# A two-layer image kernel: the LayerNorm of one image and the projection and convolution of the next, written as one stage

## The chip, the cores and the metric

The kernel runs on one core of one Trainium2 chip (trn2). The metric is the device time of one execution in microseconds (us); lower is better. Before the change the median of three runs is 33011.9 us (32997.37 to 33019.17). One execution was also recorded by the hardware profiler; it took 33035.09 us, of which 33033.3 us lie between the first and the last instruction (the span).

## What is computed

Eight images of 56x56 pixels with 192 channels pass through two layers, each of the form `x = x + layer(groupnorm(x))`. The first layer is not touched by the change. The second layer, cut to what matters here, is

```python
xz = x @ W_in.T                      # 192 -> 2*384
xc, z = split(xz, 2)                 # each 384 channels
xc = silu(depthwise_conv3x3(xc) + conv_b)
# eight directed scans over the 3136 pixels, each a recurrence with 16 states per channel
h  = exp(delta * A) * h + (delta * u) * B      ;  y_k = sum_n(h * C)
y  = sum over the 8 directions of y_k, put back in pixel order, + D * xc
y  = layernorm(y) * ln_w + ln_b
out = (y * silu(z)) @ W_out.T        # 384 -> 192
```

## The kernel before, in words

Everything is float32. After the first layer of all eight images, one loop over the images (`for b in range(B)`, L398) runs the second layer in three stages for each image. Each stage opens its own pools of on-chip memory and closes them again.

- **Preparation (L412 to L482).** The image is cut into seven tiles of 8 rows (448 pixels, `T`). For each tile the layer's input is loaded and normalised (`normed`, L400), projected to 3 blocks of 128 channels (`pp`, L432) and copied by ScalarE into a padded image `xp` (L435). Then the 3x3 depthwise convolution runs on TensorE: nine matmuls with diagonal matrices `dg` per block and tile (`pc`, L446), SiLU by ScalarE into a separate tensor `xc` (L453), a store of `xc` to DRAM (L459), and copies into the pixel orders that the scans read: `xo0` by VectorE (L470), `xo1` by GpSimd (L468), each with every second row reversed, and, once the whole image is there, the transposed order `xo2` by both (L481, L479). All are stored to DRAM (`xod`, L471, L482).
- **Scan (L485 to L923).** The long stage; its order is written by hand (`manual_schedule`, L500). VectorE runs the recurrences (L761). It is not changed. Its results go to DRAM (`ytd`, L709).
- **LayerNorm (L926 to L1040).** Again seven tiles. For each, four buffers `yk` of 112 pixels x 8 directions x 384 channels are loaded by 16 DMAs each, half issued on SP's queue and half on ScalarE's (L955, L967); three such buffers exist. TensorE transposes and adds them into `ysum` (L983, 24 instructions per buffer). VectorE adds `D*xc` (L994); TensorE forms the mean (`p1`, L999); VectorE subtracts it (L1002); ScalarE squares (L1004); TensorE forms the variance (`p2`, L1007); ScalarE takes the root (L1009), VectorE the reciprocal (L1010), then scales (L1024, L1025, L1028). TensorE forms the gate `pz` (L1014), ScalarE its SiLU (L1022). TensorE projects to 192 channels (`po`, L1032), VectorE adds the residual (L1039), SP stores the result (L1040).

In preparation and LayerNorm the framework's scheduler decides the order of the instructions on each engine; in the scan, and wherever `manual_schedule` is entered, an engine takes its instructions in the order in which the program writes them. An engine, and a queue that issues DMAs, works strictly in order: what waits holds up what stands behind it. Each DMA also waits, by a counter, for the eighth DMA before it.

A float32 matmul shows as two instructions in the trace, so 42 matmuls of `po` per image appear as 84.

Of the kernel before, what the change touches and what calls it, by code (L numbers as in the profile page):

```python
# [38 lines left out]
F32 = mybir.dt.float32  # L39
AF = mybir.ActivationFunctionType  # L40
ALU = mybir.AluOpType
# [43 lines left out]
def conv_kernel(ctx: ExitStack, tc: tile.TileContext, a: dict, out: bass.AP):  # L85
# [298 lines left out]
    xcd = [dram.tile([128, NB, L], F32, name=f"xc{b}") for b in range(B)]  # L384
# [9 lines left out]
    def halves(t):  # L394

        return t.rearrange("p d (h w) -> p d h w", w=HW)

    for b in range(B):  # L398
# [13 lines left out]
        with ExitStack() as st:  # L412
            one = st.enter_context(tc.tile_pool(name="prep1", bufs=1))
            pre = st.enter_context(tc.tile_pool(name="prep", bufs=2))
            pm = st.enter_context(tc.tile_pool(name="pp", bufs=4, space=PSUM))
            win = one.tile([CP, 2, 2 * DI], F32, name="win")
            nc.sync.dma_start(win, a["W_inT"])
            xp = [one.tile([128, HW + 2, HW + 2], F32, name=f"xp{d}") for d in range(NB)]
            dg = one.tile([128, NB, 9, 128], F32, name="dg")
            for d in range(NB):  # L420
                for edge in (xp[d][:, 0, :], xp[d][:, HW + 1, :], xp[d][:, :, 0], xp[d][:, :, HW + 1]):
                    nc.gpsimd.memset(edge, 0.0)  # L422
                for j in range(9):
                    nc.vector.tensor_scalar(
                        dg[:, d, j, :], ident, cw[:, d, j : j + 1], None, ALU.mult
                    )
            for t in range(NT):
                _, xn = normed(pre, t)
                for d in range(NB):
                    pp = pm.tile([128, T], F32, name="pp")  # L430
                    for c in range(2):
                        nc.tensor.matmul(  # L432
                            pp, win[:, c, d * 128 : (d + 1) * 128], xn[:, c], start=(c == 0), stop=(c == 1)
                        )
                    nc.scalar.copy(  # L435
                        xp[d][:, 1 + t * RT : 1 + (t + 1) * RT, 1 : HW + 1],
                        pp.rearrange("p (h w) -> p h w", w=HW),
                    )
            xc = one.tile([128, NB, L], F32, name="xc")
            xcv = xc.rearrange("p d (h w) -> p d h w", w=HW)  # L440
            for t in range(NT):
                for d in range(NB):
                    pc = pm.tile([128, RT, HW], F32, name="pc", tag="pp")
                    for j in range(9):
                        dy, dx = divmod(j, 3)
                        nc.tensor.matmul(  # L446
                            pc,
                            dg[:, d, j, :],
                            xp[d][:, t * RT + dy : t * RT + dy + RT, dx : dx + HW],
                            start=(j == 0),  # L450
                            stop=(j == 8),
                        )
                    nc.scalar.activation(  # L453
                        xc[:, d, t * T : (t + 1) * T],
                        pc.rearrange("p h w -> p (h w)"),
                        AF.Silu,
                        bias=cb[:, d : d + 1],
                    )
                nc.sync.dma_start(xcd[b][:, :, t * T : (t + 1) * T], xc[:, :, t * T : (t + 1) * T])  # L459
                for o in range(2):  # L460
                    xo = pre.tile([128, NB, T], F32, name=f"xo{o}")
                    for par in range(2):
                        src = xcv[:, :, t * RT + par : (t + 1) * RT : 2, :]
                        dst = halves(xo)[:, :, par::2, :]
                        if par != o:
                            src = src[:, :, :, ::-1]
                        if o:
                            nc.gpsimd.tensor_copy(dst, src)  # L468
                        else:
                            nc.vector.tensor_copy(dst, src)  # L470
                    nc.sync.dma_start(xod[b][o][:, :, t * T : (t + 1) * T], xo)  # L471
            xct = xcv.rearrange("p d h w -> p d w h")
            for t in range(NT):
                xo = pre.tile([128, NB, T], F32, name="xo2", tag="xo0")
                for par in range(2):
                    src = xct[:, :, t * RT + par : (t + 1) * RT : 2, :]
                    dst = halves(xo)[:, :, par::2, :]
                    if par:
                        nc.gpsimd.tensor_copy(dst, src[:, :, :, ::-1])  # L479
                    else:  # L480
                        nc.vector.tensor_copy(dst, src)  # L481
                nc.sync.dma_start(xod[b][2][:, :, t * T : (t + 1) * T], xo)  # L482
# [442 lines left out]

        with ExitStack() as st:  # L926
            one = st.enter_context(tc.tile_pool(name="ln1", bufs=1))
            wk = st.enter_context(tc.tile_pool(name="ln", bufs=2))
            pm = st.enter_context(tc.tile_pool(name="lnp", bufs=2, space=PSUM))
            py = st.enter_context(tc.tile_pool(name="lny", bufs=2, space=PSUM))  # L930
# [6 lines left out]
            for t in range(NT):  # L937
                pos = slice(t * T, (t + 1) * T)
                x1, xn = normed(wk, t)
                xc = wk.tile([128, NB, T], F32, name="xc")  # L940
                nc.sync.dma_start(xc, xcd[b][:, :, pos])

                ysum = py.tile([128, NB, 512], F32, name="ysum", tag="py")
                yv = ysum[:, :, :T].rearrange("p d (h w) -> p d h w", w=HW)
                for h0 in (0, 1, 4, 5):

                    yk = wk.tile([2 * HW, K, DI], F32, name="yk", bufs=3)
                    h = t * RT + h0
                    for place, o, rev in DIRS.values():
                        if o == 2:  # L950
                            continue
                        eng = nc.scalar if rev else nc.sync
                        for i in range(2):
                            at = (HW - 3 - h if rev else h) + 2 * i
                            eng.dma_start(  # L955
                                yk[i * HW : (i + 1) * HW, place], ytd[b][place, at * HW : (at + 1) * HW]
                            )
                    for rev in range(2):
                        for i in range(2):
                            for par in range(2):  # L960

                                at = HW + HW - 1 - h - 2 * i if par else h + 2 * i
                                if rev:
                                    at = L - 1 - (at + (HW // 2 - 1) * 2 * HW)
                                p0 = i * HW + par * (HW // 2)
                                eng = nc.scalar if rev else nc.sync
                                eng.dma_start(  # L967
                                    yk[p0 : p0 + HW // 2, 4 + 2 * rev : 6 + 2 * rev],
                                    ytd[b][
                                        4 + 2 * rev : 6 + 2 * rev, at : at + (HW // 2 - 1) * 2 * HW + 1 : 2 * HW  # L970
                                    ].rearrange("k l d -> l k d"),
                                )
                    for d in range(NB):
                        for place, o, rev in DIRS.values():
# [15 lines left out]
                            )  # L990

                y = wk.tile([128, NB, T], F32, name="y")
                for d in range(NB):
                    nc.vector.scalar_tensor_tensor(  # L994
                        y[:, d], xc[:, d], dsum[:, d : d + 1], ysum[:, d, :T], ALU.mult, ALU.add
                    )
                p1 = pm.tile([128, T], F32, name="p1", tag="pm")
                for d in range(NB):
                    nc.tensor.matmul(p1, ones, y[:, d], start=(d == 0), stop=(d == NB - 1))  # L999
                yc = wk.tile([128, NB, T], F32, name="yc")  # L1000
                for d in range(NB):
                    nc.vector.tensor_sub(yc[:, d], y[:, d], p1)  # L1002
                sq = wk.tile([128, NB, T], F32, name="sq")
                nc.scalar.activation(sq, yc, AF.Square)  # L1004
                p2 = pm.tile([128, T], F32, name="p2", tag="pm")
                for d in range(NB):
                    nc.tensor.matmul(p2, ones, sq[:, d], start=(d == 0), stop=(d == NB - 1))  # L1007
# [107 lines left out]
```

## Time and profile before

| | us |
|---|---|
| median of the runs | 33011.9 |
| profiled execution | 33035.09 |
| its span | 33033.3 |
| VectorE from the end of an image's last scan to the next image's first, seven times | 574.4 to 577.6 each |
| the last image's LayerNorm, from VectorE's last scan to the end of the span | 332 |
| TensorE, VectorE, ScalarE, GpSimd busy over the span | 30106.0, 23832.6, 23299.1, 22361.9 |

Every image shows the same pattern: some 3125 us of scan, in which all four engines are busy most of the time, and then a gap in which VectorE does no scan. The gap holds the LayerNorm of the image that was just scanned (about 329 us), then the preparation of the next one (about 206 us), then the start-up of the next scan (about 41 us). In the profile's groups of instructions, "busy" counts the time of an engine's instructions, "mean ns" is one instruction's duration (matmuls overlap each other, so their number times their mean exceeds the time that they take), and the last column is the time for which the engine idled just before them, with what ended it.

### The profile page before, as it was taken

How to read it: one execution, taken by the hardware profiler on the slowest of the kernel's cores; microseconds unless marked ns; L12 is line 12 of the kernel's file. 1: busy time of each engine (PE TensorE's matmuls, PEld its weight loads, DVE VectorE, ACT ScalarE, POOL GpSimd, SP SyncE). 2: the span in 40 equal slices, each digit the busy share in tenths (PEclk: the TensorE clock that was granted, in tenths of full speed). 3: DMA queues.
4: the chain of work that ended last, by engine and by line, in shares of the span. 5: the costliest groups of instructions: out<-in, count | busy, mean ns of one | idle time of the engine just before them, and what ended most of it. 6: DMA issues, size and time to landing. Idle time of an engine off the chain costs nothing. (4 is left out here: it accounts for less than half of the span.)

```text
span 33033.3 us, 535851 instructions
## 1 busy us (share of the span) xinstructions
PE 30106.0 (91%) x195376; PEld 20579.6 (62%) x195376; DVE 23832.6 (72%) x13236; ACT 23299.1 (71%) x63562; POOL 22361.9 (68%) x11632
## 2 busy tenths in 40 slices
PE   8999899979998899979998899979998899979998
PEld 5555566646665566646665566646665566646665
DVE  3444588848886588848886688848886688848886
ACT  2332588838886588838886688838885688838885
POOL 0000588838886588838886588838885688838885
PEclk9999999989999999989999999989999999989999
DMA  3222344444444444444444344444444344444444
GB/s 78 60 60 56 116 126 127 127 127 125 126 129 132 120 127 128 126 126 128 125 126 138 119 125 126 129 128 124 127 128 133 118 129 125 126 127 130 125 126 132
DMA packets 4719499, 3974.35 MB, mean 120 GB/s; under 512 B 3678496, under 2 KB 4401888, under 8 KB 4611008
## 3 DMA queue, kind: packets, MB, share of 16 engines
q1 hardware_dynamic: 4558272, 3778.58, 40.3%
q10 hardware_dynamic: 158592, 161.47, 1.9%
q8 instruction: 1552, 25.43, 0.3%
q14 instruction: 1083, 8.87, 0.1%
HBM read 3406.62 MB, written 547.17 MB: 120 GB/s over the span
## 5 line engine op out<-in xcount | busy, mean ns | idle before, releaser
L761 DVE TENSOR_TENSOR_SCAN h<-da,bx 128x1024 f32<-128x1024 f32 x9600 | 21447.9, 2275 | 3899.2 <-ACT bx L756 2956.6
L779 POOL TENSOR_TENSOR hc<-h,cbt 128x1016 f32<-128x1016 f32 x9600 | 20694.4, 2177 | 2470.8 <-DVE h L761 1973.9
L688 ACT ACTIVATE da<-delta,A_logs 128x254 f32<-128x254 f32 x39936 | 17115.8, 490 | 856.1 <-PE bx L733 807.1
L733 PE MATMUL bx<-bd,dut 63*128 63x252 f32 (+1 forms) x76800 | 11032.5, 404 | 1071.2 <-ACT bx L756 376.8
L789 PEld LDWEIGHTS yps<-ident,hc 128*127 128x127 f32 x76800 | 9246.5, 190 | 3384.3 <-issue 2081.0
L789 PE MATMUL yps<-ident,hc 128*127 128x128 f32 x76800 | 11065.2, 287 | 196.4 <-ACT bx L756 142.7
L733 PEld LDWEIGHTS bx<-bd,dut 63*128 63x128 f32 (+1 forms) x76800 | 6506.3, 187 | 4540.3 <-ACT da L688 878.0
L422 POOL MEMSET xp<- 128x58 f32 x96 | 10.3, 194 | 5692.5 <-DMA x<-x1d 3395.9
L612 POOL TENSOR_TENSOR du<-delta,xs 128x381 f32<-128x381 f32 x1600 | 1605.7, 1004 | 712.7 <-ACT bx L756 477.3
L1004 ACT ACTIVATE sq<-yc 128x1344 f32<-128x1344 f32 x56 | 74.0, 1322 | 2111.9 <-DMA yk<-yt 1781.2
L540 PE MATMUL px<-xs,xpw 128*64 128x508 f32 (+1 forms) x2688 | 1304.4, 576 | 226.7 <-DMA xs<-xo 198.4
L575 PE MATMUL pd<-pxs,dtw 13*128 13x508 f32 x2304 | 1296.6, 642 | 17.9 <-ACT delta L584 10.7
L584 ACT COPY delta<-pd 128x508 f32<-128x508 f32 x1152 | 669.7, 581 | 727.2 <-PE pd L575 721.4
L756 ACT COPY bx<-h 128x8 f32<-128x8 f32 x4608 | 753.2, 163 | 594.1 <-PE bx L733 324.2
L446 PE MATMUL pc<-xp,dg 128*128 128x448 f32 x3024 | 1138.0, 538 | 0.0
L774 ACT COPY carry<-h 128x8 f32<-128x8 f32 x4608 | 884.1, 192 | 320.9 <-DVE h L761 302.6
L756 ACT COPY bx<-carry 128x8 f32<-128x8 f32 x4992 | 820.4, 164 | 400.3 <-PE bx L733 369.1
L468 POOL COPY xo<-xc 128x672 f32<-128x672 f32 x112 | 80.6, 749 | 1392.8 <-issue 754.8
L699 ACT COPY yt<-yps 127x256 f32<-127x256 f32 (+1 forms) x2496 | 890.2, 357 | 175.6 <-PE yps L789 122.3
L446 PEld LDWEIGHTS pc<-xp,dg 128*128 128x128 f32 x3024 | 571.2, 189 | 565.5 <-issue 565.5
L470 DVE COPY xo<-xc 128x672 f32<-128x672 f32 x112 | 90.3, 848 | 1129.3 <-ACT xc L453 1129.3
L406 DVE TENSOR_SCALAR x1n<-x,gstat 96x448 f32<-96x448 f32 x224 | 103.6, 505 | 1078.8 <-DMA x<-x1d 803.5
(121 smaller groups left out, 17121.0 us busy)
## 6 DMA issues: line engine op xcount, KB each, us to landing
cbt<-cd SPq DMA_DIRECT2D x768, 2032.0 KB
bd<-bd SPq DMA_DIRECT2D x1600, 512.0 KB
xs<-xo SPq DMA_DIRECT2D x384, 762.0 KB
yt<-yt SPq DMA_DIRECT2D x1536, 190.5 KB
yk<-yt ACTq DMA_DIRECT2D x1792, 84.0 KB
yk<-yt SPq DMA_DIRECT2D x1792, 84.0 KB
xo<-xo SPq DMA_DIRECT2D x168, 672.0 KB
xc<-xc SPq DMA_DIRECT2D x112, 672.0 KB
```

The lines of the kernel that those rows point to most:

```text
L446: nc.tensor.matmul(pc, dg[:, d, j, :], xp[d][:, t * RT + dy : t * RT + dy + RT, dx : dx + HW], start=(j == 0), stop=(j == 8),)
L540: nc.tensor.matmul(self.px[:, : self.n], weights[self.k][0][:, d], self.xs[:, d], start=(d == 0), stop=(d == NB - 1),)
L575: nc.tensor.matmul(self.pd[:, : self.n], weights[self.k][1][:, d * 128 : (d + 1) * 128], self.pxs[0 : R + 1], start=True, stop=True,)
L612: nc.gpsimd.tensor_mul(self.du, self.delta[:, :, part], xs[:, :, part])
L688: yield nc.scalar.activation(da[:, : G.ncs, n, 1:], src.rearrange("p (c t) -> p c t", t=W), AF.Exp, scale=an[:, G.k, self.d, col : col + 1],)
L699: nc.scalar.copy(G.yt[:, : G.ncs, self.d * 128 : (self.d + 1) * 128], yps[:, self.i % 2, : G.ncs])
L733: mm = nc.tensor.matmul(self.bx[:, 4 * q : 4 * q + 4, 1 + 64 * r : 1 + 64 * r + nr], dut[rows, P.d * 128 : (P.d + 1) * 128], bd[rows, n0 : ...
L756: return nc.scalar.copy(self.bx[:, :, 0], prev)
L761: nc.vector.tensor_tensor_scan(self.h.rearrange("p n t -> p (n t)"), das[2 * (P.i % 2) + self.half][:, self.c].rearrange("p n t -> p (n t) ...
L774: nc.scalar.copy(P.carry[:, P.d, states(self.half)], self.h[:, :, W])
L779: nc.gpsimd.tensor_tensor(self.hc, self.h[:, :, 1:], G.cb[P.s][:, states(self.half), self.c * W : (self.c + 1) * W], ALU.mult,)
L789: nc.tensor.matmul(yps[:, self.P.i % 2, self.c], lhsT=self.hc[:, n], rhs=ident, start=(self.half == 0 and self.c == 0 and n == 0), stop=(s ...
```

## The change

The preparation stage remains for the first image only (`if b == 0`). The LayerNorm stage of image b now also holds the projection and the convolution of image b+1, and the whole stage stands under `manual_schedule`, so that its instructions run in the order written in the loop at its end. Besides:

- The convolution writes its result into the padded image itself, shifted by one pixel (`xcv = xp[:, :, :HW, :HW]`); the separate `xc` is gone.
- `xc` is no longer stored to DRAM (`xcd` is gone). The LayerNorm reads the order `xo0` in its place and turns every second row back while it adds, in six VectorE instructions of 224 pixels per channel block instead of three of 448.
- All loads of `yk` are issued on SP's queue; `load_y(j + 3)` is issued after the transposes of buffer j.
- The gate is formed block by block, the output projection of a tile is put into the next tile's turn, and LayerNorm works in place on `y`. In on-chip accumulator memory (PSUM) there is now one `ysum`, one bank for the two sums, two for gates and output, two for projection and convolution.

```diff
-    xcd = [dram.tile([128, NB, L], F32, name=f"xc{b}") for b in range(B)]
...
+        if b == 0:
             with ExitStack() as st:
...
+            st.enter_context(tc.manual_schedule())
+            more = b + 1 < B
...
+            class Next:
+                def load(self, t):
+                    if more and t < NT:
+                        self.xn = wk.tile([CP, 2, T], F32, name="xnext")
+                        nc.sync.dma_start(self.xn, x1d[b + 1][:, :, t * T : (t + 1) * T])
...
+                def orders(self, t):
...
+                            if o:
+                                nc.gpsimd.tensor_copy(dst, src)
+                            else:
+                                nc.vector.tensor_copy(dst, src)
+                def store(self, t):
+                    if more:
+                        for o in range(2):
+                            nc.sync.dma_start(xod[b + 1][o][:, :, t * T : (t + 1) * T], self.xo[o])
...
-                        eng = nc.scalar if rev else nc.sync
...
+                        nc.sync.dma_start(
+                            yk[i * HW : (i + 1) * HW, place], ytd[b][place, at * HW : (at + 1) * HW]
+                        )
...
+            X = Next()
+            tiles = [Tile(t) for t in range(NT + 1)]
+            X.load(0)
+            load_y(0)
+            tiles[0].load()
+            load_y(1)
+            X.normed(0)
+            X.project(0)
+            X.load(1)
+            load_y(2)
+            X.normed(1)
+            X.project(1)
+            X.load(2)
+            for t in range(NT):
+                Y, Z = tiles[t], tiles[t - 1] if t else None
+                Y.normed()
+                X.normed(t + 2)
+                Y.turn_back(0)
+                X.project(t + 2)
+                X.load(t + 3)
+                tiles[t + 1].load()
+                Y.turn_back(1)
+                X.conv(t, 0)
+                Y.gate(0)
+                Y.gate(1)
+                Y.turn_back(2)
+                Y.turn_back(3)
+                Y.with_x()
+                if Z:
+                    Z.project()
+                X.conv(t, 1)
+                Y.centre()
+                Y.gate(2)
+                if Z:
+                    Z.store()
+                X.conv(t, 2)
+                Y.scale()
+                X.orders(t)
+                X.store(t)
+            X.turned_order()
+            Y.project()
+            Y.store()
```

What the names of the loop stand for: `X` is the next image. `X.normed` is two VectorE instructions as in L406; `X.project` is the 12 instructions of L432 for one tile with three copies as in L435; `X.conv(t, d)` is one block's nine matmuls (18 instructions) as in L446 with its SiLU; `X.orders` and `X.store` are L470, L468 and L471; `X.turned_order` is L481, L479 and L482. `Y` is the tile of the present image. `turn_back(i)` is 24 instructions as in L983; `gate(d)` is one block of L1014 (4 instructions) with its SiLU; `with_x` is the six additions; `centre` is the 6 instructions of `p1`, the three subtractions and the squares; `scale` is the 6 instructions of `p2`, the root, the reciprocal and the scaling. `Z` is the tile before; `Z.project` is its 12 instructions of `po` with two additions on VectorE. For the last image `more` is false and all of `X` is empty.

## The prediction

> **What bounds the kernel now.** First the page: busy times, and VectorE (DVE) in the 40 slices.
>
> ```profile
> PE 30106.0 (91%) x195376; PEld 20579.6 (62%) x195376; DVE 23832.6 (72%) x13236; ACT 23299.1 (71%) x63562; POOL 22361.9 (68%) x11632
> ...
> DVE  3444588848886588848886688848886688848886
> ```
>
> The scan slices read 8; the slices of 4 to 6 between them are where the change works. So I went to the timeline of VectorE around the last of these gaps (start us, length us, instruction, idle before):
>
> ```profile
> 28989.57 10.97 DVE L761 TENSOR_TENSOR_SCAN h<-da,bx 128x1024 f32<-128x1024 f32 x5
> 29000.63 0.17 DVE L936 MEMSET ones<- 128x128 f32 x1
> ...
> 29533.17 1.42 DVE L481 COPY xo<-xc 128x672 f32<-128x672 f32 x1 [1.89 <-DMA xo<-xo]
> 29576.75 2.29 DVE L761 TENSOR_TENSOR_SCAN h<-da,bx 128x1024 f32<-128x1024 f32 x1 [42.16 <-ACT bx L756]
> ```
>
> One gap lasts 29000.5 to 29576.7, 576.2 us; the seven gaps differ by 3 us. The table by stretches says what TensorE (PE) does in its two parts, LayerNorm and then preparation with scan start-up (the columns are PE, weight loads, DVE, ACT, POOL busy, granted clock, DMA share, GB/s), and below them in one stretch of transposes:
>
> ```profile
> 29000.50:29329.40 328.90, 206.22 (x940) 124.19 (x940) 91.53 (x121) 40.96 (x36) 2.33 (x2) 0.80 0.56 151
> 29329.40:29576.70 247.30, 196.00 (x498) 96.01 (x498) 33.47 (x62) 37.72 (x64) 25.39 (x42) 0.85 0.35 117
> 29161.20:29168.40 7.20, 7.20 (x75) 7.02 (x73) 1.08 (x1) 0.00 (x0) 0.00 (x0) 1.00 0.54 156
> ```
>
> In LayerNorm TensorE idles 123 us and runs at a granted clock of 0.80; VectorE and ScalarE are nearly empty. The groups of TensorE in those stretches give the work:
>
> ```profile
> L983 PE MATMUL ysum<-ident,yk 112*128 112x112 f32 x672 | 73.4, 268 | 31.0 <-DMA yk<-yt 30.8 <-issue 0.2
> L1032 PE MATMUL po<-yc,wout 128*96 128x448 f32 x84 | 49.4, 759 | 59.6 <-DVE yc L1028 59.6
> L1007 PE MATMUL p<-sq,ones 128*128 128x448 f32 x42 | 29.1, 858 | 23.5 <-ACT sq L1004 23.5
> ...
> L446 PE MATMUL pc<-xp,dg 128*128 128x448 f32 x378 | 142.2, 538 | 0.0
> ```
>
> `pc` never waits: 142.2/378 = 0.376 us per instruction of 448 columns at full clock. `po` needs 49.4/84 = 0.59 because it starts slow after a wait. The timeline of one LayerNorm tile shows the chain:
>
> ```profile
> 29141.40 4.13 PE L1007 MATMUL p<-sq,ones 128*128 128x448 f32 x6 [3.19 <-ACT sq L1004]
> ...
> 29154.04 7.29 PE L1032 MATMUL po<-yc,wout 128*96 128x448 f32 x12 [8.52 <-DVE yc L1028]
> 29161.17 7.26 PE L983 MATMUL ysum<-ident,yk 112*128 112x112 f32 x74
> ```
> ```profile
> 29146.23 2.95 DVE L1010 RECIPROCAL rs<-rs 128x448 f32<-128x448 f32 x1 [6.30 <-ACT rs L1009]
> ...
> 29152.34 1.56 DVE L1028 TENSOR_TENSOR yc<-yc,sz 128x1344 f32<-128x1344 f32 x1
> ```
>
> From the end of `p2` (29145.53) to the end of the scaling (29153.90) pass 8.4 us in which TensorE does nothing; and `po`, 12 instructions, then takes 7.29 us where 12 x 0.376 = 4.5 would do. An idle spell of 8.5 us so costs 2.8 us more by the clock. Transposes take 7.26/74 = 0.098 us, 24 of them 2.35.
>
> Last, SP's queue while buffers come free one at a time:
>
> ```profile
> 29163.67 2.04 SPq L955 DMA_DIRECT2D yk<-yt  x4
> 29166.90 2.14 SPq L967 DMA_DIRECT2D yk<-yt  x4
> ```
>
> That is 0.52 us to issue one load of `yk`.
>
> **The merged tile, part by part.** TensorE's work per tile is 4 x 2.35 transposes, 4.5 projection (12), 20.3 convolution (54), 4.5 gate (12), 4.5 `po` (12), 4.5 `p1` and `p2`: 47.7 us, 334 for seven tiles, against 535 for LayerNorm and preparation (329 + 206). The waits of LayerNorm for `sq` lie under a convolution block (6.8), and the wait of `po` for the scaling under the next tile's start. That is the gain.
>
> What the written order takes back is on VectorE. At a tile's end stand, in order, the scaling of this tile, two copies of `X.orders`, `Y.normed` and `X.normed(t + 2)`; on TensorE `X.project(t + 2)` stands second in the next tile, after 2.35 us of transposes. So `X.project` waits for all of them: 8.4 (above) + 1.6 (two copies, row L470, 0.85 each, overlapped) + 0.9 + 0.9 (L406, 0.5 each) = 11.8 us after `p2`. TensorE idles 9.5 us and pays the 2.8 us of the clock again, as `po` does now. Behind the waiting projection are the second transposes, all convolutions and gates: nothing covers it. A tile with projection and a predecessor takes 47.7 + 9.5 + 2.8 = 60.0; there are four (t = 1 to 4).
>
> Tiles 5 and 6 have no projection: 43.2. There SP decides: its two `X.store` wait for the VectorE copies (10.0 after the tile's start), and `load_y` of the fourth buffer stands behind them: two stores 1.1, 16 x 0.52 = 8.3, landing 2.9 (as `out_y<-x` at 29326.40 freed its waiter at 29329.37): 22.3. TensorE is there after 3 x 2.35 + 6.8 + 3.0 = 16.9, waits 5.4, pays some 2 of clock: 50.5, two of them 101. In tiles 1 to 4 TensorE gets to that buffer only at 33, so this wait is covered by the other.
>
> Start (from the last scan): the last `yt` store lands at 13.9; weights, the first x and its norm to 21; `X.project(0)` at slow clock 7.3 to 29; `X.load(1)` stands on SP behind two buffers and two tile loads (34.5), lands 37.4, norm 38.3, `X.project(1)` slow again to 45.7; first transposes 48; `X.project(2)` 52.6; then 2.35 + 6.8 + 3.0 + 4.7 + 6.8 + 2.3 + 1.5 + 6.8 + 2.3 to 89. End: scaling and copies 10.0, seven transposed copies paced by their stores as now (29516.1 to 29534.6) 18; then a new step: the last `po` additions (1.1), the `out` store and its landing stand ahead of the scan's first load on SP, 4.4 where it was 1.0; start-up 41.2 as now. Sum 73.6. The gap becomes 89 + 240 + 101 + 73.6 = 504, 72.6 less than 576.2; seven of them: -508.
>
> The last image's LayerNorm (332 us) now has all loads on SP: 64 x 0.52 + 3 x 0.55 = 35 per tile against 41.2 (29154.04 to the next `po` at 29195.29): 6 x 6 less, some 15 more at its start, where four buffers come through one queue: -20, between -40 and +30. Sum: 33035.1 - 528 = 32507 for the profiled execution, which was 23.2 above the median: 32485.
>
> **Costs that the trace does not show.** One queue loading alone: between 0.32 us (an issue's own length) and 0.94 (at this stage's start SP issued 32 loads from 29015.63 to 29045.81, but ScalarE as many beside it). I take 0.52, since the new loop frees one buffer at a time, as that row does; even 0.88 would fit under 60 us. The six additions of 224 pixels take between 2.0 and 4.0 us (half of, or the whole of, 0.67 each); they lie under `po` and a convolution (11.3), so nothing either way. The dropped `xc` store saves SP 0.5 us per tile: nothing on the path. ScalarE has some 10 us per tile (SiLU 6 x 0.63, copies 3 x 0.54, square 1.32, root 0.63, two table loads 1.28): covered.
>
> The Trainium skill speaks against the order on one point: "TensorE: Matmul & The Clock Gate", Part 4 on PE-mode transpose, says that transposes do not count as activity for the clock gate. By that rule 4.7 us of transposes ahead of `Z.project` would let the clock fall in each tile, 2.8 us x 49 = 137 us in all. The stretch above was 7.2 us of transposes at a granted clock of 1.00, and ten `pz` instructions after it took 3.94 us (0.39 each): I count nothing; by the rule it would be 32620.
>
> **The rivals.** (1) TensorE sets the pace: if the projection did not wait, four tiles lose 12.3 us each, 344 us over seven gaps: 32140. For it: VectorE would have 17 us of work in 48. Against it: the order of instructions, in which the norm stands behind the scaling. (2) SP's pace near 0.75: start +11 (48 loads), tiles 5 and 6 +3.7 each (16 loads), seven times 18.4, and the last image +50 instead of -20: 32685. (3) Slower: one queue needs 1.0 us per load. Then SP's 64 loads and its other DMAs (3.3 us) set the tile at 67 us. With d per load the gap is 89 - 25 (48 start loads at 0.52) + 6 x 3.3 + 73.6 = 157, plus (48 + 6 x 64) d = 432 d: 589, or +13 seven times; the last image's six tiles take 65.6 each instead of 41.2, +146: about +240, 33250. It decides from d = 0.93 on. For it: 0.94 at the start; against it: 0.52 whenever ScalarE's queue is not pressing too. (4) Nothing moves because the parts still run one after another: the order of instructions excludes it almost wholly.
>
> **Chances.** Forecast (32400 to 32570) 0.62; rival 1 and what lies between, 0.10; rival 2 (32600 to 32850) 0.20; rival 3, 0.06; no change 0.02. The range 32240 to 32720 leaves out the lower half of rival 1, the upper third of rival 2, and 3 and 4. A measurement tells 0.2% (66 us) from no change: faster 0.92, same 0.03, slower 0.05.
>
> **What would show it.** In the profile after: VectorE's gap near 504; TensorE's `pp` group with some 9.5 us idle before it four times per gap, released by the norm on VectorE; the clock in the merged stage above 0.85; `ysum` waiting for `yk` only in tiles 5 and 6 and at the start; SP's loads near 0.52. Wrong if `ysum` waits for `yk` in every tile (rival 2 or 3), or if `pp` does not wait (rival 1).

## The result, and the profile after

The changed kernel takes 32435.45 us (32433.44 to 32446.73) where the kernel before took 33009.24 us in the same series: a ratio of 0.9827, 95% interval 0.981 to 0.9844. The profiled execution took 32433.44 us, 601.7 less than the one before. Seven gaps gave 542.4 of it (497.3 to 500.1 us each, where they were 574.4 to 577.5), the last image's LayerNorm 53.4 (278.6 against 332.0), the scans, whose code is the same, some 16, with a cause that stays open; the first layer, which the change does not touch, took 10.3 us more.

The page's busy times and VectorE's slices, after:

```profile
PE 29974.2 (92%) x195376; PEld 20574.4 (63%) x195376; DVE 23854.0 (74%) x13460; ACT 23290.3 (72%) x63667; POOL 22357.6 (69%) x11632
...
DVE  3444588858887588848887688848886688858886
```

They hardly differ from before: TensorE runs as many instructions. A gap of 500 us is less than one slice of 811 us, so the page can't show this change. The stretches of the last gap can (start, the four tiles with a projection, the two without, the end, and last the whole gap; the third number from the right is the granted clock):

```profile
28531.10:28619.10 88.00, 60.64 (x228) 35.21 (x229) 13.12 (x46) 12.27 (x19) 5.12 (x16) 0.81 0.58 164
28619.80:28859.30 239.50, 202.84 (x795) 117.41 (x794) 64.44 (x101) 38.13 (x53) 5.76 (x8) 0.90 0.49 143
28859.30:28960.40 101.10, 91.99 (x365) 54.76 (x363) 30.52 (x47) 15.87 (x20) 3.62 (x5) 0.93 0.37 113
28960.40:29028.90 68.50, 24.41 (x48) 9.58 (x48) 19.61 (x19) 11.91 (x21) 13.27 (x16) 0.60 0.63 191
...
28531.10:29028.90 497.80, 380.58 (x1438) 217.65 (x1438) 127.70 (x211) 78.83 (x113) 27.77 (x44) 0.85 0.50 147
```

The prediction had 89, 240, 101 and 73.6 for these four; it counted from the ends of `p2`, 0.7 us ahead of the reciprocals at which these rows begin, so that the measured end is 69.2. In the merged tiles the clock is 0.90 and 0.93, above the 0.85 that it named. TensorE idles 117 us of the gap, where it idled 174. TensorE's groups over this gap say where:

```profile
L998 PE MATMUL pc<-xp,dg 128*128 128x448 f32 x378 | 145.7, 538 | 0.0
L1123 PE MATMUL ysum<-ident,yk 112*128 112x112 f32 x672 | 73.7, 268 | 8.4 <-DMA yk<-yt 8.4
L980 PE MATMUL pp<-xnext,win 96*128 96x448 f32 x84 | 50.5, 773 | 62.8 <-DVE xnext L965 36.7 <-DMA yk<-yt 26.1
L1193 PE MATMUL po<-y,wout 128*96 128x448 f32 x84 | 35.8, 579 | 8.7 <-DVE y L1187 8.7
```

`po` waits once, at the end, and no longer in every tile (59.6 us before). The projection of the next image, `pp`, waits 36.7 us for the norm, and this is four times one wait, as TensorE's timeline shows (last column: the idle time before):

```profile
28551.07 7.71 PE L980 MATMUL pp<-xnext,win 96*128 96x448 f32 x12 [16.44 <-DMA yk<-yt]
28568.48 7.54 PE L980 MATMUL pp<-xnext,win 96*128 96x448 f32 x12 [9.70 <-DMA yk<-yt]
...
28630.57 7.23 PE L980 MATMUL pp<-xnext,win 96*128 96x448 f32 x12 [9.16 <-DVE xnext L965]
28690.03 8.22 PE L980 MATMUL pp<-xnext,win 96*128 96x448 f32 x12 [9.16 <-DVE xnext L965]
28750.47 7.02 PE L980 MATMUL pp<-xnext,win 96*128 96x448 f32 x12 [9.17 <-DVE xnext L965]
28809.72 8.11 PE L980 MATMUL pp<-xnext,win 96*128 96x448 f32 x12 [9.17 <-DVE xnext L965]
```

What stands ahead of that norm on VectorE, in the first of these tiles:

```profile
28626.17 1.56 DVE L1187 TENSOR_TENSOR y<-y,sz 128x1344 f32<-128x1344 f32 x1
28627.65 1.60 DVE L1024 COPY xo<-xp 128x672 f32<-128x672 f32 x2
28629.17 0.92 DVE L1096 TENSOR_SCALAR x1n<-x,gstat 96x448 f32<-96x448 f32 x2
...
28630.01 0.93 DVE L965 TENSOR_SCALAR xnext<-xnext,gstat 96x448 f32<-96x448 f32 x2
```

The end of the scaling, the copies, one norm, the other: `pp` begins at 28630.57, when the first half of the last one is there. In tiles 5 and 6 SP decides. SP's queue and then TensorE in tile 5 (SPq is the queue of SP):

```profile
28868.76 1.49 SPq L1029 DMA_DIRECT2D xo<-xo  x2
28870.36 5.59 SPq L1060 DMA_DIRECT2D yk<-yt  x8
28876.00 3.42 SPq L1071 DMA_DIRECT2D yk<-yt  x8
```
```profile
28875.57 0.29 PE L1123 MATMUL ysum<-ident,yk 112*128 112x112 f32 x1 [0.29 <-DMA yk<-yt]
...
28881.32 3.56 PE L1123 MATMUL ysum<-ident,yk 112*128 112x112 f32 x18 [1.19 <-DMA yk<-yt]
28884.71 4.69 PE L1193 MATMUL po<-y,wout 128*96 128x448 f32 x12
```

The loads stand behind the two stores of the next image, and the fourth transposes trickle in behind them.

### The profile page after: what moved, and what is told of

The parts are those of the page before. It is cut to its first block, busy times and chain, and to the rows that moved or that the text cites. A ratio compares the mean times of both kernels' runs of the same rounds, so it can differ in the third digit from the quotient of the medians.

```text
span 32431.7 us, 535874 instructions
## 1 busy us (share of the span) xinstructions
PE 29974.2 (92%) x195376; PEld 20574.4 (63%) x195376; DVE 23854.0 (74%) x13460; ACT 23290.3 (72%) x63667; POOL 22357.6 (69%) x11632
## 5 line engine op out<-in xcount | busy, mean ns | idle before, releaser
L732 PEld LDWEIGHTS bx<-bd,dut 64*128 64x128 f32 (+1 forms) x76800 | 6510.0, 187 | 4511.0 <-ACT da L687 876.4
L1022 POOL COPY xo<-xp 128x672 f32<-128x672 f32 x98 | 70.5, 749 | 2841.8 <-ACT xp L1005 2841.8
L1005 ACT ACTIVATE xp<-pc,conv_b 128x448 f32<-128x448 f32 x147 | 93.5, 636 | 1352.1 <-PE pc L998 1352.0
L998 PE MATMUL pc<-xp,dg 128*128 128x448 f32 x2646 | 1019.5, 538 | 0.0
L1142 DVE SCALAR_TENSOR_TENSOR y<-xc,dsum,ysum 128x224 f32<-128x224 f32 x336 | 125.4, 443 | 1132.3 <-PE ysum L1123 1132.3
L620 ACT COPY dut<-pt 127x384 f32<-127x384 f32 x1600 | 757.9, 474 | 167.5 <-PE pt L616 123.6
L616 PE MATMUL pt<-ident,du 128*127 128x128 f32 x4800 | 815.7, 279 | 52.1 <-POOL du L611 36.2
```

What stands on the lines that cost most here:

```text
L732: mm = nc.tensor.matmul(self.bx[:, 4 * q : 4 * q + 4, 1 + 64 * r : 1 + 64 * r + nr], dut[rows, P.d * 128 : (P.d + 1) * 128], bd[rows, n0 : ...
L998: nc.tensor.matmul(pc, dg[:, d, j, :], xp[:, d, t * RT + dy : t * RT + dy + RT, dx : dx + HW], start=(j == 0), stop=(j == 8),)
```

## The experiments

Theory A is the prediction's: TensorE's work is 47.7 us per merged tile, and the change gives part of its gain back at two places in in-order queues, the norm behind the scaling on VectorE and the `X` store ahead of the loads on SP. Its main rival says that another resource stands right behind (loads, VectorE's sum of work), so that moving these instructions gives nothing. The medians below are of four runs, eleven for the split loads; each stands beside runs of the kernel before on the same chip. These took between 33004.8 and 33071.9 us, so that across rows the ratios compare better than the times. Periods are from one tile's reciprocal to the next one's, in the last gap. None of the kernels changes what is computed.

| | us | ratio to before, interval | a gap (mean of seven) | tiles 1 to 4 | tiles 5, 6 | last LayerNorm |
|---|---|---|---|---|---|---|
| before | 33009.24 | 1 | 576.2 | | | 332.0 |
| the change | 32435.45 | 0.9827 (0.981 to 0.9844) | 498.7 | 59.9 | 50.6 | 278.6 |
| X's norm ahead | 32141.01 | 0.9733 (0.9719 to 0.9748) | 456.7 | 48.9 | 51.4 | 278.5 |
| two queues | 32519.06 | 0.9849 (0.9834 to 0.9863) | 505.3 | 59.9 | 49.2 | 315.9 |
| order alone | 32603.99 | 0.9874 (0.9858 to 0.9891) | 521.6 | | | 277.7 |
| X's store behind | 32364.44 | 0.9789 (0.9774 to 0.9803) | 483.3 | 59.7 | 43.1 | 277.6 |
| norms and store | 31995.69 | 0.969 (0.9675 to 0.9704) | 434.0 | 47.6 | 43.1 | 284.8 |
| start and end too | 31941.55 | 0.9676 (0.966 to 0.9692) | 428.3 | 47.6 | 43.1 | 284.7 |
| loads split | 33135.15 | 1.0021 (1.0012 to 1.003) | 565.8 | 63.9 | 63.5 | 468.8 |

**The norm of X ahead of the scaling.**

```diff
                 Y.normed()
-                X.normed(t + 2)
+                if t == 0:
+                    X.normed(2)
...
+                X.normed(t + 3)
                 Y.scale()
```

> The next image's norm of an X tile is issued on VectorE ahead of the scaling of the Y tile (the first one stays where it is), nothing else is moved. Theory A (VectorE's written order is what makes the projection wait, 9.16 us of idle time ahead of L980 in tiles 1 to 4): that wait goes, tiles 1 to 4 fall from 59.9 us to about 49 us (the 47.7 us of TensorE's work and some 1 us of wait for yk), a gap between scans from 498.7 to about 455 us, the kernel to about 32130 us. Rival R (the wait only passes on to the yk loads behind the store of X on SP's queue, or to the gate): tiles stay at 55 us or more, a gap at 480 us or more, the kernel at 32295 us or more.

32141 us, a gap of 456.7. TensorE's groups over the last gap:

```profile
L1123 PE MATMUL ysum<-ident,yk 112*128 112x112 f32 x672 | 74.6, 268 | 13.2 <-DMA yk<-yt 13.2
L980 PE MATMUL pp<-xnext,win 96*128 96x448 f32 x84 | 37.4, 600 | 28.0 <-DMA yk<-yt 17.5 <-DVE xnext L965 10.5
```

Of the 36.7 us none is left in tiles 1 to 4 (the 10.5 are at the start), and `pp` itself takes 37.4 us where it took 50.5: the slow restarts went with the waits. 11.0 us per tile, 44 in four, are the price of where two instructions of 0.5 us stood; 42.0 of them reach the gap, since tiles 5 and 6 become 0.8 us longer each. `ysum` waits only 4.8 us longer in the whole gap, so that little of the wait passed on to the loads.

**The store of X behind the next tile's loads.**

```diff
                 Y.turn_back(0)
+                if t:
+                    X.store(t - 1)
                 X.project(t + 2)
...
                 X.orders(t)
-                X.store(t)
+            X.store(NT - 1)
             X.turned_order()
```

> Only the store of X is moved, behind the first yk loads of the next tile; both norms stay behind the scaling. Theory A (two separate waits: VectorE's order in tiles 1 to 4, SP's order in tiles 5 and 6): tiles 1 to 4 stay at 60 us, tiles 5 and 6 fall from 50.5 to 44 or 45 us, a gap near 487 us, the kernel near 32350 us. Rival R (the yk wait of tiles 5 and 6 comes from the loads' own pace or from the three buffers, whatever stands ahead of them on SP): tiles 5 and 6 stay at 49 us or more, the kernel within 30 us of 32435 us.

Tiles 1 to 4 stay at 59.7, tiles 5 and 6 fall to 43.1, as much as TensorE's work. The gap is 483.3, 3.7 less than expected, for the most part because the wait in these tiles goes wholly. TensorE's groups:

```profile
L1123 PE MATMUL ysum<-ident,yk 112*128 112x112 f32 x672 | 67.5, 259 | 0.0
L980 PE MATMUL pp<-xnext,win 96*128 96x448 f32 x84 | 49.0, 753 | 63.9 <-DVE xnext L965 47.0 <-DMA yk<-yt 16.9
```

`ysum` waits for nothing, `pp` as in the change (four times 9.16 us; the other 10.4 for `xnext` lie at the start): two separate waits, each with its own place in a queue.

**Both norms and the store.** As the two above, and the next tile's `Y.normed` is also put ahead of the scaling.

```diff
-                Y.normed()
-                X.normed(t + 2)
+                if t == 0:
+                    Y.normed()
+                    X.normed(2)
                 Y.turn_back(0)
+                if t:
+                    X.store(t - 1)
...
+                X.normed(t + 3)
+                if t + 1 < NT:
+                    tiles[t + 1].normed()
                 Y.scale()
                 X.orders(t)
-                X.store(t)
+            X.store(NT - 1)
```

> Both norms (of the next X tile and of the next Y tile) are issued on VectorE ahead of the scaling, and the store of X, whose wait holds up SP's queue, is issued behind the first yk loads of the next tile. Theory A (two waits, each made by the place of one instruction in an in-order queue, stand above TensorE's 47.7 us of work): tiles 1 to 4 at about 47.7 us, tiles 5 and 6 at about 44 us, a gap near 434 us, the kernel at about 31960 us. Rival R (another resource, VectorE's sum of work or the DMA transfers, bounds a tile above TensorE): tiles 1 to 4 stay above 52 us and the kernel above 32150 us.

47.6 us for each of tiles 1 to 4 and 43.1 for 5 and 6: TensorE's work and nothing besides. The groups, and the whole gap:

```profile
L1123 PE MATMUL ysum<-ident,yk 112*128 112x112 f32 x672 | 67.5, 259 | 0.0
L980 PE MATMUL pp<-xnext,win 96*128 96x448 f32 x84 | 38.9, 621 | 28.1 <-DMA yk<-yt 16.7 <-DVE xnext L965 11.4
L1193 PE MATMUL po<-y,wout 128*96 128x448 f32 x84 | 35.3, 572 | 8.7 <-DVE y L1187 8.7
```
```profile
28144.90:28580.80 435.90, 361.45 (x1438) 208.70 (x1438) 127.91 (x211) 78.94 (x113) 28.02 (x44) 0.90 0.57 168
```

All waits left lie at the start and at the end. The same 1438 instructions keep TensorE busy for 361 us instead of 381, at a granted clock of 0.90 instead of 0.85. VectorE, busy 128 us of 436, bounds none of these tiles. The gap is as estimated, the median 36 us above the estimate: seven gaps shorter by 64.7 from 32435 make 31982, not 31960, and a first layer 8 us and a last LayerNorm 6 us longer than in the change make the rest. In that LayerNorm nothing is gained (see its part below).

**Start and end too.** Beyond the edits above:

```diff
-                        self.xn = wk.tile([CP, 2, T], F32, name="xnext")
+                        self.xn = wk.tile([CP, 2, T], F32, name="xnext", bufs=3)
...
-                def turned_order(self):
+                def turned_order(self, last):
...
+                        if t == 4:
+                            last.project()
+                            last.store()
...
             X.load(0)
+            X.load(1)
...
-            X.turned_order()
-            Y.project()
-            Y.store()
+            X.turned_order(Y)
```

> The kernel with both norms ahead of the scaling and the later store of X, and more: a third buffer for the loaded X tile, so that X tiles 0 and 1 are loaded first and the projection of tile 1 runs while the first yk loads are on their way; X tile 2's load ahead of the third tile's yk loads; and the last Y tile's projection issued after the fifth turned copy instead of after all of them. Theory A (start and end of the gap each hold 10 us or so in which TensorE waits for loads, or copies wait for nothing): a gap shorter by 5 to 15 us than with the two norms and the store moved, the kernel at 31880 to 31960 us. Rival R (start and end are set by the transfers themselves and by the turned loads' waits on VectorE, so order gains nothing more): 31980 us or more.

31941.55 us, the fastest of these kernels, 3.2% below the kernel before and 54 us below the kernel with norms and store (on another chip, where before was 18 us lower too). The gap shortens by 5.7 us, near the lower end of what A said; seven times that is 40: the start goes from 90.9 to 82.5 us in the last gap, and the end stays (68.6 and 68.3 us). So A holds for the start and the rival for the end. SP's queue there:

```profile
28500.41 0.33 SPq L1208 DMA_DIRECT2D out_y<-x  x1
28501.70 2.07 SPq L1046 DMA_DIRECT2D xo<-xo  x2
28508.97 0.61 SPq L522 DMA_DIRECT2D xpw<-in_x_proj  x1
```

The result's store is now ahead of the last two turned stores, and still the scan's first load is issued only 5.2 us after the last of those: it now waits 4.9 us for that one to land.

**The order alone.** Every image is prepared in a stage of its own, as the first one; nothing is merged. (The convolution then writes a tensor of its own, as for the first image; in this the text of the expectation is not what ran.)

```diff
-        if b == 0:
+        if b >= 0:
...
-            more = b + 1 < B
+            more = False
```

> The written order and the in-place convolution stay, but nothing is merged: the projection and convolution of every image is a stage of its own, as for the first image, ahead of its scans, and the LayerNorm runs in the written order alone, as for the last image. Theory A (the order alone is worth what it gave in the last image, 279 us of LayerNorm instead of 332 us, eight times; the merge itself only gives the remaining some 25 us a gap): about 32600 us, gaps near 523 us. Rival R (the gain is the merging of two stages, TensorE's work laid beside the norm's): gaps near 570 us, the kernel at 32950 us or more.

32603.99 us, 32590.59 to 32616.17: as expected of A. Of the 77.5 us that a gap lost by the change, 54.7 come without any merging, from a LayerNorm in the written order with its loads on one queue (the dropped store of `xc` and the other small changes are in it too; no run takes them apart); merging as the change does it adds 22.8. It would be worth more (434.0 against 521.6) once its two waits are gone.

**Two queues.** The loads of the turned places go back to ScalarE's queue.

```diff
-                        nc.sync.dma_start(
+                        (nc.scalar if rev else nc.sync).dma_start(
```

The same at both loads.

> The loads of the turned places go back to ScalarE's queue, as in the kernel before; the rest of the change stays. Theory A (one queue carries all loads without limiting tiles 1 to 4, and only some 5 us in tiles 5 and 6 and at the start come from it, while ScalarE then pays for issuing 8 loads a tile ahead of its copies and gate): 32400 to 32520 us. Rival R (the single queue is a cost that the change took on): 32300 us or less, with tiles 5 and 6 near 45 us.

32519.06 us: the single queue is a gain, not a cost. In the merged stage tiles 5 and 6 gain 2.8 us together (52.7 and 45.6), but the start loses 14. In the last image's LayerNorm, which goes from 278.6 to 315.9 us, ScalarE's waits show how. In the change, and then with two queues (us in all, times, longest):

```profile
ACT sq L1158 <- DVE y L1156: 97.7, 7, 18.1
...
ACT L1172 <- DMA yk<-yt: 33.8, 1, 33.8
```
```profile
ACT L1172 <- DMA yk<-yt: 129.8, 6, 46.4
ACT sq L1158 <- DMA yk<-yt: 78.1, 6, 16.3
```

With loads on its own queue ScalarE reaches its gates and squares only when the loads ahead of them could be issued, and the tile waits for ScalarE: TensorE waits 37.7 us for the squares in this LayerNorm, where it waited 11.6 in the change, and a tile takes 36.8 us on average, against 32.5.

**Every load split in two.**

```diff
-                        nc.sync.dma_start(
-                            yk[i * HW : (i + 1) * HW, place], ytd[b][place, at * HW : (at + 1) * HW]
-                        )
+                        for c in (slice(0, DI // 2), slice(DI // 2, DI)):
+                            nc.sync.dma_start(
+                                yk[i * HW : (i + 1) * HW, place, c],
+                                ytd[b][place, at * HW : (at + 1) * HW, c],
+                            )
```

The loads of the turned order are cut likewise, one place at a time.

> Every yk load is cut into two of half its bytes, so that SP issues 128 a tile instead of 64; nothing else is changed and the same bytes are moved. Theory A (a load costs SP some 0.42 us whatever its size, so that SP needs 54 us and 3 us for its other DMAs per tile): the last image's tiles go from 32.5 to about 57 us, in the merged stage tiles 1 to 4 stay within 60 to 64 us (SP still fits under the wait on VectorE's order), tiles 5 and 6 go to 57 us, the start of the gap grows by some 20 us, the kernel to 32750 to 33000 us. Rival R (SP's cost goes with the bytes or the pieces of a load, so that two halves cost what one whole does): 32400 to 32550 us, the last image's tiles at 34 us or less.

33135.15 us, 0.2% slower than the kernel before on its chip (33071.89). A load costs SP the same at half the bytes. SP's queue in the merged stage:

```profile
29164.77 6.79 SPq L1074 DMA_DIRECT2D yk<-yt  x16
```

That is 0.424 us for each, where the whole loads took 3.42/8 = 0.428. The mechanism is A's. That smaller pieces made the transfers the limit does not fit: in the last image's tiles the DMA engines are busy 0.44 of the time, where they were 0.67 in the change, and SP waits only 19.4 of 360 us. But the time lies 135 us above A's bound: the last image's tiles take 60.0 us (57 expected), tiles 5 and 6 63.5 (57), the start 22.6 more (20), and the chip is a slower one (the kernel before took 63 us more on it than in the series of the change). The sum took SP to issue at an even pace. Right behind stores and tile loads it doesn't: 16 loads take 9.16 or 10.58 us there instead of 6.79.

## Why the prediction was right

**VectorE's order.** Right in place and size: 9.16 us four times against 9.5, a restart of 2.5 to 3.7 us against 2.8, tiles of 59.9 against 60.0. Undoing it gave 42.0 us per gap; the prediction's 12.3 a tile would have made 49. The missing part is a wait of about 1 us for `yk` that comes out once the larger one is gone, 48.9 instead of 47.7, and 0.8 us more in tiles 5 and 6 each.

**SP in tiles 5 and 6.** 50.4 and 50.7 us against 50.5, and with the store moved 43.1, the prediction's 43.2 for TensorE's work. But the sum is right by luck in its parts: whole bursts go at 0.42 us per load and not at 0.52, while the eight loads right behind the stores took 5.59 us, 0.70 each. So the 16 loads took 9.1 us instead of 8.3, and the last of them landed some 1.9 us later instead of 2.9.

**The start.** 88.0 us against 89, its two slow projections at 7.71 and 7.54 against 7.3.

**The end.** 69.2 us against 73.6. The scaling and copies took 10.0 as put. The mis-sized term is the seven turned copies: 14.3 instead of 18. VectorE's timeline before, and then in the change:

```profile
29523.21 1.41 DVE L481 COPY xo<-xc 128x672 f32<-128x672 f32 x1 [2.03 <-DMA xo<-xo]
29524.87 1.42 DVE L481 COPY xo<-xc 128x672 f32<-128x672 f32 x1 [0.26 <-DMA xo<-xo]
```
```profile
28975.33 1.33 DVE L1043 COPY xo<-xp 128x672 f32<-128x672 f32 x1 [0.50 <-DMA xo<-xo]
28977.21 1.34 DVE L1043 COPY xo<-xp 128x672 f32<-128x672 f32 x1 [0.54 <-DMA xo<-xo]
```

In the change they stand 1.8 us apart. Before, they came in pairs, with about 2 us of wait ahead of every other one: there the pool had two such buffers; the change gives this tile three (`bufs=3`), which the prediction had overlooked. That the third buffer makes the difference is read from these lines; no run varies it.

The rest, 44.9 us to the first scan, was put at 45.6 (4.4 and 41.2), and here two errors cancel: from the last copy to the scan's first load it took 5.7 us, and from there to the first scan 39.1. The cause of the new step is the one predicted, the landing of the result's store. What SP waits for ahead of the scan's first load, in the change and then with start and end too (us in all, times, longest):

```profile
SPq L522 <- DMA out_y<-x: 4.0, 1, 4.0
```
```profile
SPq L522 <- DMA xo<-xo: 4.9, 1, 4.9
```

With the result's store out of the way, the load waits as long for the last turned store, so that the end did not get shorter. In the kernel before, the load followed the last turned store by 0.4 us (29535.18 to 29535.57) and waited for no landing.

**The last LayerNorm.** This step failed: -53.4 where it said -20, between -40 and +30. Two terms were wrong. The start was to lose 15 us to one queue; it gained 1.5 (64.3 from 65.8), and it is with two queues that it takes 75.1. And the tiles, put at 35 us by SP's 0.52 a load, took 32.5: at 0.42 the same sum is 64 x 0.42 + 3 x 0.55 = 28.5, and SP's waits add 3.3 a tile. Nor were the loads what TensorE waited for. Its waits in these six tiles of the change, and then one of those with both norms and the store moved:

```profile
PE z L1165 <- DVE x1n L1096: 26.6, 6, 4.5
PE ysum L1123 <- DMA yk<-yt: 1.8, 1, 1.8
```
```profile
PE ysum L1123 <- DMA yk<-yt: 26.1, 28, 1.7
```

(Another 10.1 us, in both, are for the squares.) The gate waits for the tile's own norm, which stands behind the scaling of the tile before, as X's norm does in the merged stage. With that norm moved ahead the wait passes on to the loads, and a tile takes 33.7 us: here the rival holds, and SP's queue stands right behind VectorE's order.

Six periods gave 50.7 us and not 36. The single queue was booked as a cost to be bounded; ScalarE, which it sets free, was not booked at all. By the run with two queues that is 37 us of the 53.

**The sum.** Seven gaps at -77.5 instead of -72.6 make 34 us, the last LayerNorm 33, the scans 16 that no step had, the first layer 10 the other way (both unexplained): 73 us, by which the profiled execution lay below 32507. The median lies 50 below the forecast, since the profiled execution after was 2 us below its median, and the one before 23 above.

**The clock and the transposes.** In the change `po` follows 4.77 us of transposes directly. The stretch of these transposes, and that of `po` after them:

```profile
28649.70:28654.30 4.60, 4.60 (x49) 4.56 (x48) 0.00 (x0) 0.54 (x1) 0.00 (x0) 1.00 0.69 199
28654.30:28659.10 4.80, 4.80 (x16) 2.22 (x14) 2.90 (x8) 0.00 (x0) 0.00 (x0) 1.00 0.60 172
```

The granted clock is 1.00 in both, and `po` took 4.68 us, where the prediction put 4.5 at full clock. The Trainium skill says in "TensorE: Matmul & The Clock Gate", Part 4, that transpose mode doesn't count as busy for the clock gate in the same way as other matmuls; by that the prediction would have been 32620. The measurement decides: here transposes of this length cost nothing.

**The rivals.** TensorE's pace (32140 in the prediction) is what the kernel has with X's norm ahead: 32141. That it fits to 1 us is luck: the tiles take 48.9 us there and not 47.7, and the 50 us by which the change lies below the forecast make up for it. The slow single queue exists, but far off: the split loads, SP's 0.85 us per former load, end 0.2% above the kernel before. The prediction's sum had put that point at 0.93; by this run it is below 0.85.

## What to carry to other kernels

Before an order is written by hand, list for each instruction that releases the bounding engine what stands ahead of it in its own queue: here two instructions of 0.5 us, behind 10 us of scaling and copies, cost 42 us per gap, and two stores ahead of loads another 15. Then look what stands right behind: in the last LayerNorm the same move gained nothing, since the loads were as late. A load cost its queue 0.42 us whether it moved 84 KB or 42, and on ScalarE's queue the loads also held up its squares and gates, 37 us in one LayerNorm; both belong in the sum, with both signs. Merging two stages pays what the order inside it allows: as first written it gave 23 us per gap over the ordered stages side by side, with two waits moved 88.

## What the runs showed of the hardware

In unbroken bursts a load costs SP 0.42 to 0.43 us at 84 KB and at half of that. A wait of 9 us on TensorE costs 2.5 to 3.7 us more in the 12 matmul instructions behind it; without such waits the granted clock of the gap rose from 0.85 to 0.90 and TensorE was busy 19 us less with the same instructions. The first scan began 10 us later in the change, and 10 to 23 us later in the other kernels, than before, although the first layer is the same code in all of them. In the change 9 of the 10 us are there after 800 us; the cause stays open.
